# Scores of the first key block in two halves of 64 keys on four square tiles of TensorE

## The chip, the cores and the metric

The kernel runs on one core of one Trainium2 chip. The metric is the device time of one execution in microseconds. The kernel before was run three times: median 3692.19 us, from 3688.66 to 3693.34 us. A separate execution was profiled, and all views below are of that one.

## The reference, cut to what matters

The input is 32 sequences of 256 tokens with 256 channels. A conditioned state-space layer (projection, short convolution, a recurrence over the 256 tokens, gate, projection) is followed by two transformer layers of local attention and a gated feed-forward part. The change lies in the attention:

```python
        def local_attention(q, k, v):
            b, h, n, d = q.shape
            w = n // WINDOW
            ...
            sim = jnp.einsum('bhwid,bhwjd->bhwij', bq, bk)
            i = bt[:, :, None]
            j = btk[:, None, :]
            mask = (i < j) | (i > j + WINDOW) | (j == -1)
            sim = jnp.where(mask, -jnp.finfo(sim.dtype).max, sim)
            attn = jax.nn.softmax(sim, axis=-1)
            out = jnp.einsum('bhwij,bhwjd->bhwid', attn, bv)
```

There are 8 heads of 64 channels and WINDOW is 128, so the 256 tokens form two windows. A query `i` sees a key `j` only where `j <= i <= j + 128`. The first key block (keys 0 to 127) is therefore seen by queries of both windows, but its first half (keys 0 to 63) by queries 0 to 191 alone, and its second half (keys 64 to 127) by queries 64 to 255 alone. The second key block (keys 128 to 255) is seen by queries 128 to 255 alone.

## The kernel before, in words

The 32 sequences are handled in four groups of eight. For each group a scan runs over the 256 tokens (`group_scan`, line 376 on): every step is one VectorE operation `h` (L706), which needs a row block `xrep` that was fetched by a transfer on SP's queue (L675) and scaled by ScalarE (L696). Four steps are read out together by TensorE, each on its own tile of 32 columns (`y`, L718). The scan of a group runs beside the attention and feed-forward work of the group before it. The last group's attention and feed-forward have no scan beside them.

The order of the transformer work is written out by hand: `attend` and `feed` put the steps of each sequence into numbered stages (`stage(n, i, ...)`, eight stages per sequence), and a loop at the end of `program` plays the stages and advances the scan slot by slot between them. The build then arranges the instructions of each engine, so that an engine's queue is nearly, and not exactly, in this order. [...]

For each sequence the attention does this. `project` makes q, k and v of a window (L965). `turn` transposes q and k, so that in `qT` and `kT` the 64 channels of an even head lie in partitions 0 to 63 and those of the odd head beside it in partitions 64 to 127. `scores` takes a key block `kw`, a first head pair `i0` and a number `n` of head pairs; it makes keys-by-queries scores in two PSUM banks, one for the even heads (`r` = 0) and one for the odd (`r` = 1). The matmuls of `r` = 0 and `r` = 1 use the upper and lower 64 rows of the array, so they are two row tiles of 64 x 128. For the first key block it is called twice per sequence (stages 3 and 5), with two head pairs and 256 queries each; for the second once (stage 2), with four head pairs and 128 queries.

The mask comes in one of two ways. In the first three groups `self.apart` is false: a bf16 matmul of an identity with the mask (L1167) opens each bank with -32768 at every hidden place and 0 elsewhere, and the score matmuls (L1174) add to it. In the last group `self.apart` is true: the score matmuls write the bank themselves, and VectorE or GpSimd multiplies by a mask of ones and zeros after the exponential. In both ways ScalarE takes the exponential of the whole bank (L1183), 128 partitions by 512, into `pT`. `sums` (L1204, four column tiles of 32) and `values` (L1223, two column tiles of 64) then read `pT`.

A matmul on fp32 operands leaves two MATMUL records and two weight loads in the trace.

## Time and profile before

| What | Value |
|---|---|
| Median of three runs | 3692.19 us (3688.66 to 3693.34) |
| Span of the profiled execution | 3693.9 us |
| TensorE busy | 3580.5 us, 97%, 19804 matmul records |
| VectorE busy | 2714.2 us, 73% |
| ScalarE busy | 2163.0 us, 59% |
| GpSimd busy | 1812.1 us, 49% |
| Score matmuls of the first key block (L1174, 64x256) | 1024 records, 147.0 us busy, 406 ns mean |
| Score matmuls of the second key block (L1174, 64x128) | 1024 records, 74.4 us busy, 285 ns mean |
| Mask matmuls (L1167) | 288 records, 88.1 us busy, 383 ns mean |

The profiled execution's own time is its span, the time from the first to the last instruction; it is within 2 us of the median of the runs. Busy time counts moments in which an engine has at least one instruction in flight; TensorE overlaps its matmuls, and where two tiles of the array work together their records overlap too, so that a record's duration is longer than the time that it adds. The page divides the span into 40 slices of about 92 us and gives the busy share of each in tenths.

### The profile page before, as it was taken

What the parts mean: (1) busy time and instruction counts of PE and PEld (TensorE: products, weight loads), DVE (VectorE), ACT (ScalarE), POOL (GpSimd) and SP (SyncE); (2) the same over time, 40 slices, a digit from 0 to 9 for tenths busy, and PEclk for the clock granted to TensorE, in tenths of its full rate; (3) what the DMA queues carried; (4) which work ended last, traced back from release to release, by engine and by line L of the source; (5) the groups of instructions that cost most, each with busy time, mean ns of one, the idle gap of its engine ahead of it and who ended that gap; (6) DMA issues with size and microseconds to landing.
All of it is one profiled execution on the core that took longest, in us unless ns stands there. A gap on an engine that the chain in (4) does not pass through costs nothing.

```text
span 3693.9 us, 56916 instructions
## 1 busy us (share of the span) xinstructions
PE 3580.5 (97%) x19804; PEld 2234.3 (60%) x19804; DVE 2714.2 (73%) x5177; ACT 2163.0 (59%) x3689; POOL 1812.1 (49%) x1745
## 2 busy tenths in 40 slices
PE   7999989999999999999999999999999999999999
PEld 4444335666566566666666666666666666666666
DVE  5888889878787777877787778877777445455553
ACT  3666656666666666666666666666666444444442
POOL 4433366445455455545455556544554444444551
PEclk9999999999999999999999999999999999999999
DMA  7877655544454555444454555544453212011101
GB/s 196 209 201 206 185 164 148 134 110 135 124 139 119 140 141 145 131 112 124 119 138 124 135 145 138 134 111 130 111 134 114 59 35 59 12 30 39 30 27 36
DMA packets 469213, 435.80 MB, mean 118 GB/s; under 512 B 228835, under 2 KB 308532, under 8 KB 468788
## 3 DMA queue, kind: packets, MB, share of 16 engines
q1 hardware_dynamic: 384466, 420.05, 42.2%
q10 hardware_dynamic: 84450, 12.01, 2.1%
q8 instruction: 160, 2.62, 0.3%
q14 instruction: 137, 1.12, 0.1%
HBM read 383.70 MB, written 46.66 MB: 117 GB/s over the span
## 4 chain that ended last, share of the span: by engine, by line
PE 67%; DVE 15%; DMA 5%; POOL 5%; ACT 3%; issue 3%; SPq 0%; ACTq 0%; DVEq 0%; POOLq 0%
PE ps_qkv L965 13%; PE pa L1326 13%; PE po_f L1354 8%; DVE h L706 6%; PE y L718 5%; PE ps_wo L1015 4%; PE sc L1174 4%; DMA xrep<-xnd 4%; PE ov L1223 3%; PE ps_out L796 3%; PE ps_in L398 2%; PE tr_qk L1004 2%; DVE acc L488 2%; PE rs L1204 2%; ACT xrep L696 2%
## 5 line engine op out<-in xcount | busy, mean ns | idle before, releaser
L706 DVE CUSTOM_DVE_ANT_0 h<-h,xrep,lim 128x512 f32<-128x512 f32 x1024 | 947.3, 925 | 232.2 <-ACT xrep L696 197.5
L696 ACT ACTIVATE xrep<-xrep,beta 128x512 f32<-128x512 f32 x960 | 672.8, 719 | 336.1 <-DMA xrep<-xnd 239.0
L965 PE MATMUL ps_qkv<-qkv,res 128*128 128x512 f32 x1536 | 724.7, 607 | 19.2 <-DVE ag L1342 8.3
L1326 PE MATMUL pa<-hT,w 128*128 128x256 f32 (+1 forms) x3072 | 690.4, 387 | 1.6 <-ACT hT L1305 1.3
L1326 PEld LDWEIGHTS pa<-hT,w 128*128 128x128 f32 (+1 forms) x3072 | 493.8, 178 | 186.6 <-issue 77.8
L989 POOL TENSOR_TENSOR rot<-rot,swp 128x512 f32<-128x512 f32 x256 | 335.4, 1310 | 482.4 <-DVE swp L986 353.2
L965 PEld LDWEIGHTS ps_qkv<-qkv,res 128*128 128x128 f32 x1536 | 278.0, 191 | 328.9 <-issue 250.0
L997 POOL TENSOR_TENSOR rn<-ss,neg_half 128x8 f32<-128x8 f32 x256 | 459.2, 1794 | 15.6 <-DVE ss L995 5.4
L1354 PE MATMUL po_f<-ag,w 128*128 128x256 f32 (+1 forms) x1536 | 388.5, 394 | 11.5 <-DVE ag L1342 7.6
L1342 DVE SCALAR_TENSOR_TENSOR ag<-pa,b_sb,ag 128x256 f32<-128x256 f32 (+1 forms) x448 | 213.1, 476 | 234.4 <-ACT ag L1334 231.8
L718 PE MATMUL y<-h,ly 128*32 128x512 f32 x2048 | 357.1, 614 | 10.7 <-DVE h L706 7.9
L1279 POOL TENSOR_TENSOR rstd<-ve,neg_half 128x2 f32<-128x2 f32 x64 | 46.4, 724 | 614.8 <-DVE ve L1277 596.9
L1354 PEld LDWEIGHTS po_f<-ag,w 128*128 128x128 f32 (+1 forms) x1536 | 273.4, 189 | 119.5 <-issue 47.3
L998 POOL TENSOR_TENSOR rot<-rot,rn 128x512 f32<-128x512 f32 x256 | 291.0, 1137 | 20.1
L978 ACT ACTIVATE sq<-ps_qkv 128x512 f32<-128x512 f32 x256 | 151.9, 596 | 229.3 <-PE ps_qkv L965 181.0
L1334 ACT ACTIVATE ag<-pa,b_sb 128x256 f32<-128x256 f32 x320 | 150.4, 470 | 206.1 <-PE pa L1326 203.6
L488 DVE SCALAR_TENSOR_TENSOR acc<-xr,wc_sb,acc 128x256 f32<-128x256 f32 x384 | 192.7, 524 | 55.7 <-POOL acc L477 55.1
L1015 PE MATMUL ps_wo<-oT,wo 128*128 128x256 f32 x1024 | 231.7, 379 | 0.3 <-ACT ag L1334 0.2
L981 DVE TENSOR_TENSOR rot<-ps_qkv,rc_sb 128x512 f32<-128x512 f32 x256 | 174.8, 683 | 73.4 <-ACT sq L978 72.3
L1174 PE MATMUL sc<-qT,kT 64*128 64x128 f32 (+1 forms) x2048 | 221.3, 345 | 0.0
L1183 ACT ACTIVATE pT<-sc 128x512 f32<-128x512 f32 x384 | 208.6, 596 | 15.2 <-PE sc L1174 13.2
L1015 PEld LDWEIGHTS ps_wo<-oT,wo 128*128 128x128 f32 x1024 | 194.3, 190 | 28.2 <-ACT ag L1334 1.0
(153 smaller groups left out, 5493.7 us busy)
## 6 DMA issues: line engine op xcount, KB each, us to landing
xrep<-xnd SPq DMA_DIRECT2D x960, 256.0 KB
rb<-inv SPq DMA_DIRECT2D x128, 256.0 KB
xnd<-xn SPq DMA_DIRECT2D x64, 256.0 KB
qkv<-in_wqkv_dram SPq DMA_DIRECT2D x24, 512.0 KB
ahead<-xs_a SPq DMA_DIRECT2D x48, 256.0 KB
xp<-ahead SPq DMA_DIRECT2D x48, 256.0 KB
xd<-xnd SPq DMA_DIRECT2D x192, 64.0 KB
w<-in_w_dram SPq DMA_DIRECT2D x80, 128.0 KB
```

What stands on the lines that cost most here:

```text
L488: nc.vector.scalar_tensor_tensor(acc, xr[:, :, k : k + CH], wc_sb[:, ch, k : k + 1], acc, ALU.mult, ALU.add,)
L696: scaled = nc.scalar.activation(bx, ck[c].pop(("bx", t), bx), AF.Copy, scale=ck[c]["beta"][:, t : t + 1])
L706: nc.vector._custom_dve(TENSOR_ADD_SAT, out=h_new, in0=state["h"], in1=bx, s0=ck[c]["lim"][:, 0, t : t + 1], s1=ck[c]["lim"][:, 1, t : t + 1],
L718: nc.tensor.matmul(ck[c]["y", hb][32 * q : 32 * q + 32, :], ly[hb % 2][:, 32 * t : 32 * t + 32], ck[c].pop(("h", hb * TB + t)), start=(i = ...
L965: nc.tensor.matmul(ps, res[b][:, k, t0 : t0 + W], wt["qkv", a][:, k], start=(k == 0), stop=(k == KM - 1),)
L989: nc.gpsimd.tensor_add(rot, rot, swp)
L997: nc.gpsimd.tensor_tensor(rn, ss, neg_half, ALU.pow)
L998: nc.gpsimd.tensor_mul(rot, rot, bc(rn, 2, DH))
L1015: nc.tensor.matmul(po[:, d], wt["wo", 0][:, c, d * P : (d + 1) * P], oT[:, c, :], start=(c == 0), stop=(c == NC_ - 1),)
L1174: nc.tensor.matmul(banks[r][:, i, :], kT[rows, i0 + i, kw * W : (kw + 1) * W], qT[rows, i0 + i, kw * W :], start=self.apart, stop=self.apa ...
L1326: nc.tensor.matmul(pg if x else pa, wt["w1", m][:, k, x], self.h[:, k], start=(k == 0), stop=(k == KM - 1),)
L1354: nc.tensor.matmul(self.po[:, d], wt["w2", 0][r0 : r0 + n, m, d * P : (d + 1) * P], self.ag[m][r0 : r0 + n], start=(m == 0), stop=(m == le ...
```

## The change

In `scores`, for the first key block and where the mask was added by TensorE, each matmul of 128 keys by 256 queries is replaced by two matmuls. The first takes keys 0 to 63 with queries 0 to 191 and writes partitions 0 to 63 of the bank; the second takes keys 64 to 127 with queries 64 to 255 and writes partitions 64 to 127. Together with the two row halves (even and odd heads) this addresses the array as four tiles of 64 x 64. The places that no matmul adds to any more (keys 0 to 63 with queries 192 to 255, and keys 64 to 127 with queries 0 to 63) are hidden ones, and keep the mask value that the mask matmul wrote. The second key block and the last group run as before. In the changed file the score matmul stands in line 1181, and later lines are seven further down.

```diff
+                halved = kw == 0 and not self.apart
+                nm = 2 if halved else 1
+                mk = W // nm
                 for i in range(n):
                     for r in range(2):
                         rows = slice(r * DH, (r + 1) * DH)
-                        nc.tensor.matmul(
-                            banks[r][:, i, :],
-                            kT[rows, i0 + i, kw * W : (kw + 1) * W],
-                            qT[rows, i0 + i, kw * W :],
-                            start=self.apart,
-                            stop=self.apart or i == n - 1,
-                        )
+                        for m in range(nm):
+
+                            k0 = m * mk
+                            q0, q1 = (k0, k0 + W + mk) if halved else (0, nq)
+                            nc.tensor.matmul(
+                                banks[r][k0 : k0 + mk, i, q0:q1],
+                                kT[rows, i0 + i, kw * W + k0 : kw * W + k0 + mk],
+                                qT[rows, i0 + i, kw * W + q0 : kw * W + q1],
+                                start=self.apart,
+                                stop=self.apart or i == n - 1,
+                            )
                 for r in range(2):
```

## The prediction

> **What bounds the kernel now.** I read the page first: the busy shares, the chain of waits, the slices.

> ```profile
> span 3693.9 us, 56916 instructions
> PE 3580.5 (97%) x19804; PEld 2234.3 (60%) x19804; DVE 2714.2 (73%) x5177; ACT 2163.0 (59%) x3689; POOL 1812.1 (49%) x1745
> ...
> PE   7999989999999999999999999999999999999999
> PEclk9999999999999999999999999999999999999999
> ...
> PE 67%; DVE 15%; DMA 5%; POOL 5%; ACT 3%; issue 3%; SPq 0%; ACTq 0%; DVEq 0%; POOLq 0%
> ```

> TensorE is busy almost throughout and holds 67% of the chain; no other engine passes 73%. A busy TensorE includes modelled ends, so I checked the part that the change touches with the view of busy time by stretches. The first score block of 256 queries starts at 535 us, and the groups with an added mask end by 2995 us:

> ```profile
> 532.00:1500.00 968.00, 935.64 (x5373) 0.99 0.50 132
> 1500.00:2995.00 1495.00, 1481.88 (x8582) 1.00 0.45 120
> ```

> TensorE idles 32.4 of 968 us in the first stretch (3.3%) and 13.1 of 1495 us in the second (0.9%). Its longest named waits there are for VectorE, 8.3 us at most in sum for one pair. So TensorE sets the pace, tightly in the second stretch, less so in the first.

> Next the groups of the view by form, and one block in the timeline, cut into stretches of 0.2 us so that records in flight together are listed apart (start us, length us, engine, line, form, count):

> ```profile
> L1174 PE MATMUL sc<-qT,kT 64*128 64x256 f32 x1024 | 147.0, 406 | 0.0
> ...
> 1508.18 0.49 PE L1174 MATMUL sc<-qT,kT 64*128 64x256 f32 x2
> 1508.50 0.81 PE L1174 MATMUL sc<-qT,kT 64*128 64x256 f32 x6
> 1508.93 0.38 PE L1174 MATMUL sc<-qT,kT 64*128 64x256 f32 x2
> 1509.24 0.64 PE L718 MATMUL y<-h,ly 128*32 128x512 f32 x4
> 1509.69 0.61 PE L718 MATMUL y<-h,ly 128*32 128x512 f32 x4
> 1510.24 0.48 PE L1326 MATMUL pa<-hT,w 128*128 128x256 f32 x1
> ...
> 1518.87 1.51 PE L1204 MATMUL rs<-pT,head_cols 128*32 128x256 f32 x32
> 1520.31 3.17 PE L1223 MATMUL ov<-pT,v_sb 128*64 128x256 f32 x32
> ```

> Each fp32 matmul leaves two records[...] (8 for the four score matmuls of a block, 2048 for the 1024 read-outs `y`, one a scan step). The block of four matmuls costs 1508.18 to 1509.24 = 1.06 us from its first record to the next work; the single records show that all 96 blocks of the masked groups have a median of 1064 ns. Two records, one per row tile, start 6 ns apart and run together. The read-out `y` shows the same for four column tiles: eight 512-column records in 1.00 us, where one after another they would take 8 x 0.427 = 3.4 us. There is no idle time before the group: operands are there.

> [...]

> **A formula for a block.** Within `sc`, single records show the second pair 320 ns after the first, further pairs 215 ns apart, and the next work 306 ns after the last record. So a pass of 256 columns takes 213 ns, the first weight load (128 columns) adds 107, a change of mode adds 93. For four 32-column tiles of 512 the second group comes 453 ns after the first: 427 + 27. For the two 64-column tiles of `ov` it comes 266 later: 213 + 53. The exposed load follows the columns of one tile, and tiles load side by side. Check on `rs`: 27 + 4 x 216 + 4 x 109 + 20 stagger + 94 = 1441 ns, and the timeline has 1518.87 to 1520.31 = 1.44 us.

> **The change, part by part.**

> *Removed and added on TensorE.* 96 blocks (3 groups x 2 layers x 8 sequences x 2) lose four matmuls 64x256 and gain eight 64x192 on four tiles: 768 more records and as many weight loads. A pass of 192 columns lies between 109 (128) and 216 (256): 162 ns. A new block, if the four tiles run together: 53 (first load, 64 columns) + 4 groups x 162 + 20 (stagger) + 94 (mode) = 815 ns. Gain 1064 - 815 = 249 ns a block, 23.9 us in all. Issue is no bound on this: `rs` issues four 128-column matmuls with their loads per 109 ns, here there are 162 ns for four. The bounds of the untried: best, also the 53 and the stagger hide, 740 ns, gain 31 us; worst, the two column halves of a row tile run in turn, 8 x 163 + 53 + 94 = 1451 ns, loss 387 ns a block, 37 us. I take 815, since both kinds of packing are seen and share one array.

> *Mask and exp.* The mask matmul (L1167) still opens the whole bank, so a corner no longer added to keeps -32768, exp of which is 0. Mode changes stay: before, the block already stood between a full-array mask matmul and other full- or column-tile work. Exp (L1183) reads the same 128x512 bank, 0.25 us earlier; it is of no use to it, as it waited only 17.6 us for scores in the whole span. No wait is added: both built programs have 3021 matmuls that wait. Not touched: the first 532 us and the last group (32 blocks after 2995 us).

> *Order.* Elsewhere the built programs stand in nearly the same order. On TensorE six instructions move; they cut `y` runs (306 runs after, 303 before). A run cut off costs its own two passes, 2 x 427 + 27 + 94 = 975 ns[...]: 3 x 1.0 to 1.2 = about 3 us. On VectorE some 119 of 5180 instructions stand elsewhere, by a few places, on ScalarE 42, GpSimd 57, on SP's queue 44, nearly all transfers of scan rows `xrep`. They are issued in the same number; I cost this at nothing, covered by TensorE's backlog, and give it 3 us either way.

> *What of it reaches the end.* A saving passes until TensorE meets a wait that doesn't move with it. In 1500 to 2995 us, 59 blocks, idle 0.9%: I take 90%: 59 x 0.249 x 0.9 = 13.2 us. In 532 to 1500 us, 37 blocks, idle 3.3%: VectorE's scan chain (waits `h` <- `xrep` <- transfer) paces some of it; I take 65%: 37 x 0.249 x 0.65 = 6.0 us. Sum 19.2, less 2.5 for order: 16.7 us. From the profiled span 3693.9 this gives 3677.2. The three runs have a median of 3692.2, 1.7 below the profiled execution, so 3675.5; I say 3675.

> **Rivals.**

> *The gain is swallowed.* VectorE (some 400 of 500 us busy between 1000 and 2500) or the scan rows' transfers become the pace; TensorE's idle grows by most of 23.9 us. For it: the chain of waits between 1490 and 1533 us runs through VectorE, GpSimd, a transfer and ScalarE without TensorE. Against: in that stretch TensorE itself had hardly a gap. A third of the gain, 8 us less 3 for order: about 3687.

> *The column halves run in turn.* In each row tile, the second half waits for the first. Place: the new block at each of 96 sites. Price 387 ns each, 3692 + 37 = 3729. It decides from a block of 1064 + 77 = 1141 ns up (7.4 us over 96), that is a group of four in 243 ns instead of 162. For it: no trace shows a row and a column split at once. Against: `y` streams four different operands from all 128 partitions into four tiles at full pace, more than this needs.

> *The order loses more than I count.* Shifted scan transfers or a later VectorE step open waits of some 15 to 20 us more than counted: 3692 to 3697, no change.

> **How the numbers follow.** Main case 0.70, around 3675, own range 3665 to 3684. Swallowed 0.14 (3684 to 3691). In turn 0.09 (3729). Order 0.07. 0.2% is 7.4 us, about what a measurement of this kernel can tell from no change: 3685 and 3700 are the bounds. Faster: 0.70 and nearly half of the swallowed, 0.76. Same: the rest of it and most of the order case, 0.13. Slower: 0.11. The range 3664 to 3690 leaves out the case in turn, some of the order case, and a full pass-through with all loads hidden (3692 - 31 = 3661).

> **What would show it.** Right: 20572 matmul records; a group of form 64*64, 64x192, x1536; four of its records starting within some 25 ns, groups 162 ns apart, a block in about 0.82 us; the gain lying between 532 and 2995 us, the time from there to the end unchanged near 699 us; TensorE idle in 532 to 2995 us up from 45.5 to about 50 us. Wrong: blocks near 1.45 us (in turn), or blocks of 0.82 us with idle up by 15 us or more (swallowed).

## The result, and the profile after

The changed kernel takes 3676.17 us in the median of five runs (3672.99 to 3681.02); the kernel before took 3691.43 us in five runs (3688.66 to 3693.34). The ratio is 0.9959, with a 95% interval of 0.9948 to 0.9970: 15 us faster. The profiled execution of the changed kernel spans 3679.2 us, and is the slowest of its five runs.

The page after, the parts that answer to those shown of before (span; busy times; slices of TensorE and its clock; the chain):

```profile
span 3679.2 us, 58433 instructions
PE 3560.8 (97%) x20572; PEld 2218.3 (60%) x20572; DVE 2708.4 (74%) x5177; ACT 2161.1 (59%) x3689; POOL 1819.4 (49%) x1745
...
PE   7999989999999999999999999999999999999999
PEclk8999999999999999999999999999999999999999
...
PE 66%; DVE 16%; DMA 5%; POOL 5%; ACT 4%; issue 3%; SPq 0%; ACTq 0%; DVEq 0%; POOLq 0%
```

TensorE's busy time fell by 19.7 us, the busy time of VectorE, ScalarE and GpSimd moved by less than 8, and the chain shifted by one point from TensorE to VectorE and ScalarE. TensorE, busy for 97% of the span and with 66% of the chain, is still the engine that sets the pace.

The new matmuls in the view by form, and one block in the timeline, cut into short stretches so that records in flight together are listed apart (start us, length us, engine, line, form, count):

```profile
L1181 PE MATMUL sc<-qT,kT 64*64 64x192 f32 x1536 | 85.9, 339 | 0.0
...
1501.56 0.39 PE L1181 MATMUL sc<-qT,kT 64*64 64x192 f32 x4
1501.78 0.67 PE L1181 MATMUL sc<-qT,kT 64*64 64x192 f32 x12
1502.10 0.34 PE L1181 MATMUL sc<-qT,kT 64*64 64x192 f32 x4
1502.37 0.64 PE L718 MATMUL y<-h,ly 128*32 128x512 f32 x4
```

Four records start together at 1501.56, on the four tiles; the last four start at 1502.10, and the next work at 1502.37, 0.81 us after the block began. Over the 96 blocks the single records give a median of 811 ns, where it was 1064. From first record to next work the 96 blocks took 105.6 us in the trace before and 80.4 us in this one: TensorE got 25 us back in these places, and the span fell by 14.7.

**Where the rest went.** TensorE's queue holds the same matmuls in nearly the same order in both kernels, so the start of each can be set against its start before. How far ahead the changed kernel is, at the same score matmul:

| Time in the kernel before, us | 533 | 669 | 1276 | 1500 | 1997 | 2975 | end |
|---|---|---|---|---|---|---|---|
| Ahead by, us | 1.0 | -2.9 | 5.1 | 6.8 | 8.5 | 14.2 | 14.7 |

Each block gains 0.25 us. Between 533 and 669 us nearly 4 us are lost all the same, and from 1276 us on, where 68 blocks give back 17.2 us, only 9.6 arrive. The last 699 us are the same in both (TensorE busy 691.4 us after, 691.1 before).

The early loss is one stall, at 622 us (timeline after, TensorE; in brackets the idle time before it and what ended it):

```profile
622.03 1.92 PE L718 MATMUL y<-h,ly 128*32 128x512 f32 x2 [4.31 <-DVE h L706]
```

A read-out of the scan waits 4.31 us for the scan step that it reads. In the kernel before no read-out waits longer than 0.5 us between 600 and 640 us. This read-out is one of the few TensorE instructions that the build moved: it was cut off from its run and put behind the mask matmuls. The place of the read-out isn't what costs, though: it stands later in TensorE's queue than before, and still waits. The step that it reads was moved too, on VectorE. Before, then after (VectorE; `rot` belongs to the rotation of q and k):

```profile
614.57 0.80 DVE L706 CUSTOM_DVE_ANT_0 h<-h,xrep,lim 128x512 f32<-128x512 f32 x1
615.29 0.68 DVE L981 TENSOR_TENSOR rot<-ps_qkv,rc_sb 128x512 f32<-128x512 f32 x1
```

```profile
616.20 0.69 DVE L981 TENSOR_TENSOR rot<-ps_qkv,rc_sb 128x512 f32<-128x512 f32 x1 [0.84 <-ACT sq L978]
...
619.23 0.69 DVE L981 TENSOR_TENSOR rot<-ps_qkv,rc_sb 128x512 f32<-128x512 f32 x1 [1.09 <-ACT sq L978]
...
621.17 0.81 DVE L706 CUSTOM_DVE_ANT_0 h<-h,xrep,lim 128x512 f32<-128x512 f32 x1
```

Before, the step `h` runs ahead of the rotations; after, it stands behind two of them in VectorE's queue, which themselves wait for ScalarE, and it ends at 621.98 us. Behind the stall TensorE is also slow for a while: the next block takes 1.48 us (623.88 to 625.36) in place of 0.81, and the mean granted clock from 532 to 680 us is 0.94, where it was 0.98.

The steady loss shows in the waits of TensorE between 1276 and 2985 us (who waited for whom: us in total, times, longest). Before, then after:

```profile
PE ps_qkv L965 <- DVE ag L1342: 8.3, 12, 1.2
PE sc L1167 <- DVE ag L1342: 4.7, 7, 0.9
PE ps_qkv L965 <- DVE rinv L1212: 1.9, 3, 0.9
```

```profile
PE ps_qkv L965 <- DVE ag L1349: 8.0, 11, 0.9
PE sc L1167 <- DVE ag L1349: 6.7, 8, 1.0
PE ps_qkv L965 <- DVE rinv L1219: 3.1, 6, 0.9
```

These are waits for a PSUM bank: the kernel passes TensorE's results through eight PSUM tiles in turn (`ps_w`, `bufs=8`), and in the program a mask matmul or a projection into a tile depends on VectorE's reading of the tile's last contents (`ag`, `rinv`). One of them in the timeline after (VectorE and TensorE):

```profile
2019.81 0.47 DVE L488 SCALAR_TENSOR_TENSOR acc<-xr,wc_sb,acc 128x256 f32<-128x256 f32 x1
2019.83 0.38 PE L1167 MATMUL sc<-mask_t,ident_b 128*128 128x512 bf16 x1
...
2020.39 0.42 DVE L471 TENSOR_TENSOR xr<-xp,cond_sb 128x256 f32<-128x256 f32 x1
2020.73 0.48 DVE L1349 SCALAR_TENSOR_TENSOR ag<-pa,b_sb,ag 128x256 f32<-128x256 f32 x1
...
2021.26 0.38 PE L1167 MATMUL sc<-mask_t,ident_b 128*128 128x512 bf16 x1 [1.05 <-DVE ag L1349]
```

The second mask matmul of the block stands 1.05 us and starts at 2021.26, when `ag` has emptied its bank (2020.73 + 0.48 = 2021.21), and `ag` stands in VectorE's queue behind the convolution of the scan's next chunk. At the same place before, TensorE came later and waited 0.6 us. TensorE's waits in this stretch grew by 4 us in all; starts that slip by 0.1 to 0.3 us inside the modelled end of the previous matmul, mostly at the second half of `values`, account for most of the other 3 to 4. That TensorE waits longer because it arrives earlier is one reading of this. It doesn't fit every wait: see the waits of `two` and `wide` below.

### The profile page after: what moved, and what is told of

It reads as the page before. It is cut to its first block, busy times and chain, and to the rows that moved or that the text cites. A ratio compares the mean times of both kernels' runs of the same rounds, so it can differ in the third digit from the quotient of the medians.

```text
span 3679.2 us, 58433 instructions
## 1 busy us (share of the span) xinstructions
PE 3560.8 (97%) x20572; PEld 2218.3 (60%) x20572; DVE 2708.4 (74%) x5177; ACT 2161.1 (59%) x3689; POOL 1819.4 (49%) x1745
## 2 busy tenths in 40 slices
PE   7999989999999999999999999999999999999999
## 4 chain that ended last, share of the span: by engine, by line
PE 66%; DVE 16%; DMA 5%; POOL 5%; ACT 4%; issue 3%; SPq 0%; ACTq 0%; DVEq 0%; POOLq 0%
PE ps_qkv L965 14%; PE pa L1333 13%; PE po_f L1361 7%; DVE h L706 6%; PE y L718 5%; PE ps_wo L1015 4%; DMA xrep<-xnd 4%; PE sc L1181 4%; PE ov L1230 4%; PE ps_out L796 3%; PE ps_in L398 2%; PE tr_qk L1004 2%; DVE acc L488 2%; PE rs L1211 2%; ACT xrep L696 2%
## 5 line engine op out<-in xcount | busy, mean ns | idle before, releaser
L696 ACT ACTIVATE xrep<-xrep,beta 128x512 f32<-128x512 f32 x960 | 673.4, 719 | 342.3 <-DMA xrep<-xnd 245.5
L718 PE MATMUL y<-h,ly 128*32 128x512 f32 x2048 | 358.1, 611 | 14.6 <-DVE h L706 13.0
L1015 PE MATMUL ps_wo<-oT,wo 128*128 128x256 f32 x1024 | 231.7, 379 | 0.5 <-ACT ag L1341 0.5
L1015 PEld LDWEIGHTS ps_wo<-oT,wo 128*128 128x128 f32 x1024 | 194.3, 190 | 28.4 <-ACT ag L1341 1.2
L1181 PE MATMUL sc<-qT,kT 64*64 64x192 f32 (+2 forms) x2816 | 196.6, 325 | 0.0
```

The lines of the kernel that those rows point to most:

```text
L696: scaled = nc.scalar.activation(bx, ck[c].pop(("bx", t), bx), AF.Copy, scale=ck[c]["beta"][:, t : t + 1])
L718: nc.tensor.matmul(ck[c]["y", hb][32 * q : 32 * q + 32, :], ly[hb % 2][:, 32 * t : 32 * t + 32], ck[c].pop(("h", hb * TB + t)), start=(i = ...
L1015: nc.tensor.matmul(po[:, d], wt["wo", 0][:, c, d * P : (d + 1) * P], oT[:, c, :], start=(c == 0), stop=(c == NC_ - 1),)
L1181: nc.tensor.matmul(banks[r][k0 : k0 + mk, i, q0:q1], kT[rows, i0 + i, kw * W + k0 : kw * W + k0 + mk], qT[rows, i0 + i, kw * W + q0 : kw * ...
```

## The experiments

Ratios are to the kernel before, run on the same chip between the runs, with 95% intervals.

| Run | What it is | Median us | Ratio | Block, ns |
|---|---|---|---|---|
| the change | halves on four tiles | 3676.2 | 0.9959 (0.9948 to 0.9970) | 811 |
| late | halves from the fourth sequence on | 3674.2 | 0.9952 (0.9939 to 0.9966) | 811 |
| two | fewer queries only (leaves out scores that are needed) | 3674.8 | 0.9950 (0.9936 to 0.9964) | 851 |
| wide | four tiles only | 3694.7 | 1.0006 (0.9998 to 1.0014) | 1024 |
| quarters | eight tiles, 160 queries | 3667.9 | 0.9935 (0.9921 to 0.9948) | 704 |
| relief_before | kernel before, less work on VectorE (leaves out one convolution tap and the reciprocal) | 3682.7 | 0.9976 (0.9968 to 0.9983) | 1064 |
| relief_after | the change, the same left out | 3660.7 | 0.9911 (0.9897 to 0.9925) | 811 |
| turns | the change, tile by tile | 3691.5 | 0.9997 (0.9987 to 1.0007) | 831 |
| before_turns | kernel before, in that order | 3725.9 | 1.0080 (1.0066 to 1.0094) | 1071 |
| before_turns_fix | the same, ScalarE's queue put in order | 3664.8 | 0.9921 (0.9907 to 0.9934) | 1071 |
| turns_fix | turns, the same | 3653.8 | 0.9897 (0.9882 to 0.9913) | 831 |
| tail | quarters, halves in the last group too | 3654.7 | 0.9897 (0.9884 to 0.9910) | 704 and 811 |
| tail_fix | tail, ScalarE's queue put in order | 3632.7 | 0.9839 (0.9825 to 0.9852) | 704 and 811 |

### What shortens a block: fewer columns or more tiles

```diff
 two:
-                nm = 2 if halved else 1
+                nm = 1
-                            q0, q1 = (k0, k0 + W + mk) if halved else (0, nq)
+                            q0, q1 = 0, nq - 64 if halved else nq
 wide:
-                            q0, q1 = (k0, k0 + W + mk) if halved else (0, nq)
+                            q0, q1 = 0, nq
 quarters:
-                nm = 2 if halved else 1
+                nm = 4 if halved else 1
```

> Only the queries are cut: 128 keys with queries 0 to 191 on the two row tiles of before (the scores of keys 64 to 127 with queries 192 to 255 are left out and stay at the mask's 0). Theory (the gain comes from 192 columns in place of 256, the four tiles are only what makes this possible): a block in 107 + 4 x 162 + 7 + 94 = 856 ns, TensorE saves 20 us, about 3679 us. Rival (the gain comes from the number of tiles at work): a block stays near 1064 ns and the time near 3691 us.

> Only the tiles are split: 64 keys with all 256 queries on four square tiles. Theory: a block in 53 + 4 x 216 + 20 + 94 = 1031 ns, 33 ns less than before, TensorE saves 3 us, 3689 to 3691 us. Rival (four tiles at work gain by themselves): a block near 811 ns and the time near 3676 us.

> The split is taken further: four quarters of 32 keys with 160 queries each, on eight tiles of 64 x 32. Theory: a pass of 160 columns takes 135 ns, a block 27 + 4 x 135 + 47 stagger + 94 = 708 ns, 103 ns less than in halves, TensorE saves 10 us more, of which some 60% pass: about 3670 us. Rival (the rate of issue bounds it, as four records and their loads take 109 ns in the row sums): groups of eight every 218 ns, a block in 27 + 4 x 218 + 47 + 94 = 1040 ns, time near 3690 us.

The forms of the new matmuls in `two`, `wide` and `quarters`, one line from each view by form:

```profile
L1181 PE MATMUL sc<-qT,kT 64*128 64x192 f32 x768 | 90.4, 355 | 0.0
```

```profile
L1181 PE MATMUL sc<-qT,kT 64*64 64x256 f32 x1536 | 106.5, 393 | 0.0
```

```profile
L1181 PE MATMUL sc<-qT,kT 64*32 64x160 f32 x3072 | 75.4, 306 | 0.0
```

The blocks came out at 851, 1024 and 704 ns, where the formula of the prediction gave 856, 1031 and 708. So the gain of a block is that of the columns: cutting the queries alone, without more tiles, gives 213 of the 253 ns; the four tiles alone give 40, which in the formula is the shorter first weight load (54) less the longer stagger (13). The tiles are there so that no score that is needed is left out, as some are in `two`. The eight tiles of `quarters` ran together as well: the eight records of a group start 7 ns apart, and the groups follow at 136 ns. The rival for `quarters`, groups every 218 ns by a bound on issue, is out.

In the whole time the three don't follow their blocks so neatly. From 1276 us on, by the start times in one profiled execution each, `two` keeps 12.7 us of 68 x 0.213 = 14.5, `quarters` 18.5 of 24.5, the change 9.6 of 17.2, and `wide` loses 1.6 where it should gain 2.7. Their queues differ from that of the changed kernel, by some 40 to 100 instructions on VectorE and by up to some 20 on ScalarE. This was the first sign that the order there is worth several microseconds. The mask matmul's wait for `ag` between 1276 and 2960 us says the same: it is 4.7 us before and 6.7 in the changed kernel, but 4.4 in `two`, which gains nearly as much in each block, and 6.2 in `wide`, which gains next to nothing. So this wait doesn't follow the gain; the order on VectorE is a rival cause for this part of the loss, and no run here holds it fixed.

### The moved instructions

```diff
-                halved = kw == 0 and not self.apart
+                halved = kw == 0 and not self.apart and self.n >= 3
```

(`self.n` is the number of the sequence.)

> The halves are used from the fourth sequence on (90 blocks instead of 96); TensorE's queue then stands exactly as before, apart from the score matmuls. Theory (the six moved TensorE instructions, a read-out put ahead of others, cost some 4 us between 532 and 680 us): no stall of several us near 618 us, start of the eighth sequence about 2 us ahead of before where the changed kernel is 3 us behind, and 3672 to 3674 us in all. Rival (that loss is chance[...]): the six blocks less cost 1.5 us, 3677 to 3678 us.

The stall is not there: between 600 and 640 us the longest wait of a read-out is 0.5 us, and from 533 to 669 us `late` gains 0.3 us against the kernel before where the change loses 3.9. The same stall, 2.7 to 4.5 us, stands at 617 to 622 us in `two`, `wide`, `quarters`, `turns` and `tail`, which have the read-out moved too. In these five too the scan step runs behind both rotations. So the traces show that the loss goes with the move of the step and of its read-out; `late` undoes both at once. The medians of 3674.2 and 3676.2 us have intervals that overlap, so in the whole time it isn't resolved. The start of the eighth sequence was no good test: `late` was already 4.2 us behind at 533 us, ahead of its first score block. Where nothing was changed, executions of these kernels lie from 4.2 us behind to 6.0 us ahead at that point, so one trace alone is good for no less than some 5 us up to there.

### Who takes the steady loss

```diff
-                for k in range(1, TAPS):
+                for k in range(1, TAPS - 1):
                     nc.vector.scalar_tensor_tensor(
...
-                nc.vector.reciprocal(rinv, rs)
+                nc.vector.tensor_copy(rinv, rs)
```

> The kernel before with less work on VectorE: the last of three convolution taps is left out and the reciprocal of the softmax sums is a plain copy, so the values differ; some 150 us of VectorE's 2714 fall away. It is the base for the run after it: below the kernel before by what its waits for VectorE cost, 3660 to 3685 us. By itself it tells nothing between the theories.

> The changed kernel with the same work left out. Theory (in the steady stretch the gain is lost where TensorE, now earlier, waits for a PSUM bank that VectorE gives back late, since VectorE's queue is nearly full there): against the base the difference grows from 15 us to 20 to 24 us, and from 1276 to 2975 us before most of 64 x 0.253 = 16 us passes instead of 9. Rival (the loss has nothing to do with VectorE): the difference stays near 15 us, and 9 of 16 pass.

The pair differs by 3682.7 - 3660.7 = 22.0 us, and from 1276 us on the two traces draw apart by 17.3 us, all that 68 blocks give. The waits of TensorE in that stretch of `relief_after`:

```profile
PE ps_qkv L965 <- DVE ag L1349: 7.1, 10, 0.9
PE ps_wo L1015 <- ACT ag L1341: 2.7, 5, 1.2
PE ps_qkv L965 <- ACT oT L1237: 1.8, 5, 0.7
PE ps_qkv L965 <- DVE swp L986: 1.0, 1, 1.0
```

No mask matmul (L1167) waits any more, and no projection for `rinv`, in either of the two. In this pair the whole gain arrives; in the changed kernel 44% of it is lost in this stretch, while `two` loses 12% and `quarters` 24%. The pair doesn't say how much of that is VectorE's load: leaving work out also made the build arrange the queues anew. Against the kernel before, some 400 instructions on VectorE, 70 on ScalarE and 50 matmuls stand elsewhere in `relief_before`. Note that the relief itself brought the kernel before only 10 us for some 150 us of VectorE's work: VectorE isn't the pace, it is late at some hand-overs.

### The order of the matmuls in a block

```diff
-                for i in range(n):
-                    for r in range(2):
+                order = [(i, r, m) for i in range(n) for r in range(2) for m in range(nm)]
+                if halved:
+                    order.sort(key=lambda x: x[1:])
+                for i, r, m in order:
```

> The changed kernel with the score matmuls of a block in another order: both head pairs of one tile, then the next tile. Theory (tiles run together only while the queue brings different tiles in a row): a tile's four passes come one after another and little runs together, a block of up to 53 + 16 x 162 + 94 = 2.7 us, which would add up to 180 us; with half of it together, some 70 us. Rival (TensorE takes a free tile's matmul from further back): a block stays at 811 ns and the time near 3676 us.

The block is 831 ns: the rival was right on this. Four passes (a pass here is one of the two records that a matmul leaves) still start together, 13 ns apart, though the fourth tile's first pass stands twelve passes further back in the queue. By these times (16 passes of 162 ns one after another would take 2.6 us) work for a free tile was taken from there. But the time is 3691.5 us, and of 22 us nothing arrives. TensorE's queue is that of the changed kernel apart from the order within these blocks. Its waits between 1276 and 2960 us:

```profile
PE ps_qkv L965 <- DVE ag L1352: 11.5, 12, 1.6
PE tr_qk L1004 <- DVE ag L1352: 11.2, 12, 1.2
PE sc L1167 <- DVE ag L1352: 6.3, 7, 1.0
```

The second line is new. I took it first for an effect of VectorE's order, since in the built program 30 of 448 products `ag` stand on the other side of a scan step, and tested whether it needs the four tiles at all:

```diff
 before_turns, against turns:
-                nm = 2 if halved else 1
+                nm = 1
-                            q0, q1 = (k0, k0 + W + mk) if halved else (0, nq)
+                            q0, q1 = 0, nq
```

> The kernel before, its score matmuls of 128 keys by 256 queries unsplit, in the order of the run turns (both head pairs of the even heads, then of the odd). TensorE's queue is otherwise as before; on VectorE 32 of the 448 feed-forward products stand on the other side of a scan step, as in turns. Theory (in turns the place of those products behind a scan step, which waits for its row, cost the whole gain): TensorE waits for `ag` at the transposes L1004 for 10 to 14 us between 1276 and 2985 us, and the time is 3702 to 3708 us. Rival (the loss in turns has to do with the four tiles): no such waits, blocks 10 to 30 ns longer, 3692 to 3695 us.

It needs no tiles: 3725.9 us, 30 us slower than the kernel before with blocks 7 ns longer, twice what I expected. The transposes wait 10.7 us for `ag`, as foretold, and the projections a further 21.7 us for `rinv`. The place of `ag` doesn't explain that, so I looked at what `ag` itself waits for. At one of these transposes in `turns` (timeline: ScalarE, VectorE, TensorE):

```profile
2038.22 0.72 ACT L696 ACTIVATE xrep<-xrep,beta 128x512 f32<-128x512 f32 x1 [2.40 <-DMA xrep<-xnd]
2038.85 0.56 ACT L1009 COPY qT<-tr_qk 128x512 f32<-128x512 f32 x1
2039.32 0.58 ACT L1009 COPY kT<-tr_qk 128x512 f32<-128x512 f32 x1
...
2040.42 0.47 ACT L1344 ACTIVATE ag<-pa,b_sb 128x256 f32<-128x256 f32 x1
2040.56 0.81 DVE L706 CUSTOM_DVE_ANT_0 h<-h,xrep,lim 128x512 f32<-128x512 f32 x1 [4.55 <-ACT xrep L696]
...
2041.28 0.48 DVE L1352 SCALAR_TENSOR_TENSOR ag<-pa,b_sb,ag 128x256 f32<-128x256 f32 x1
...
2041.91 0.63 PE L1004 MATMUL tr_qk<-ident,rot 128*128 128x128 f32 x4 [1.13 <-DVE ag L1352]
```

and at the same place in the changed kernel:

```profile
2034.65 0.56 ACT L1009 COPY qT<-tr_qk 128x512 f32<-128x512 f32 x1
2035.12 0.59 ACT L1009 COPY kT<-tr_qk 128x512 f32<-128x512 f32 x1
2035.59 0.73 ACT L696 ACTIVATE xrep<-xrep,beta 128x512 f32<-128x512 f32 x1
2037.16 0.72 ACT L696 ACTIVATE xrep<-xrep,beta 128x512 f32<-128x512 f32 x1 [0.84 <-DMA xrep<-xnd]
2037.79 0.46 ACT L1341 ACTIVATE ag<-pa,b_sb 128x256 f32<-128x256 f32 x1
```

In `turns` ScalarE's queue has the scaling of a scan row ahead of the copies of q and k. The row's transfer isn't there, ScalarE stands for 2.40 us, and the copies, which free two banks, and the Gelu `ag`, on which VectorE's `ag` waits, stand behind it. In the changed kernel the copies come first. VectorE's order has a smaller part in it: `ag` could have started when ScalarE's Gelu ended at 2040.89, and started at 2041.28, behind the scan step. In the built programs 30 of the 256 copies stand behind one row more than in the kernel before in `turns`, 28 in `before_turns`, and 2 in the changed kernel. So I held the rows back: in the next edit each scaling of a row depends on the last copy that the kernel's text puts ahead of it (an edge for the build, which then can't put the row first).

```diff
 turn():
-            nc.scalar.copy(dst, tr)
+            last_copy[0] = nc.scalar.copy(dst, tr)
 scale_row():
                     tc.keep_in_program_order(scaled)
+                    if last_copy[0] is not None:
+                        tc.add_manual_dep(
+                            scaled.ins, last_copy[0].ins.name,
+                            mybir.DependencyInfo(
+                                mybir.DependencyClass.NoSync, mybir.DependencyReason.DATA
+                            ),
+                            reason="behind the copies",
+                        )
```

> As before_turns, but on ScalarE every scaling of a scan row (L696) stays behind the copies of q and k that the kernel's text puts ahead of it; in before_turns 28 of the 256 copies stand behind one row scaling more than in the kernel before, here none does, and 157 stand further ahead. TensorE's queue is otherwise the same. Theory (before_turns lost 30 us since ScalarE, waiting for a row's transfer, held back the copies that free TensorE's banks): 3680 to 3700 us, and the waits of the transposes L1004 for `ag` gone. Rival (another of the moved instructions is the cause, on VectorE): 3715 us or more.

> As turns, with the same rule on ScalarE. Theory: the gain of the shorter blocks arrives, 3660 to 3680 us. Rival: it stays near 3691 us.

3725.9 became 3664.8 us, and 3691.5 became 3653.8: both below the changed kernel. ScalarE's waits for a row's transfer between 1276 and 2960 us were 87.8 us before and 95.5 us in the changed kernel; in `before_turns`:

```profile
ACT xrep L696 <- DMA xrep<-xnd: 142.4, 42, 5.8
```

In `before_turns_fix` no such wait is left among the waits of that stretch, and TensorE's are these three:

```profile
PE sc L1177 <- DVE ag L1362: 4.8, 7, 1.3
PE ov L1243 <- DVE ag L1362: 0.7, 2, 0.4
PE ps_wo L1025 <- ACT ag L1354: 0.2, 1, 0.2
```

So holding the rows back on ScalarE is enough to undo what `before_turns` lost, and the timelines show how a row ahead of the copies does harm. That ScalarE's order alone is the cause isn't shown. The edge names ScalarE only, but the build followed it on VectorE: by the traces some 160 instructions stand elsewhere there, and in the built programs 16 of the 448 products `ag` stand behind one scan step more than in the kernel before in `before_turns`, and none in `before_turns_fix`. The edge also does more than undo the loss: 157 copies now stand ahead of rows that they stood behind in the kernel before, and the kernel gains 28 us with blocks of the old size. What the edge doesn't restore is the passing of the gain. Between `before_turns_fix` and `turns_fix` lie 11.0 us, and their blocks differ by 96 x 0.240 = 23 us, so half is lost here too. The wait of the mask matmul for `ag` grows from 4.8 to 6.8 us; where the rest of this loss lies isn't shown.

### A faster version

```diff
 tail, against the change:
-                halved = kw == 0 and not self.apart
-                nm = 2 if halved else 1
+                halved = kw == 0
+                nm = (2 if self.apart else 4) if halved else 1
...
-                    nc.scalar.activation(p, banks[r], AF.Exp)
+                    if self.apart and halved:
+                        for m in range(nm):
+                            k0, q0 = m * mk, m * mk
+                            s = slice(k0, k0 + mk), slice(None), slice(q0, q0 + W + mk)
+                            nc.scalar.activation(p[s], banks[r][s], AF.Exp)
+                    else:
+                        nc.scalar.activation(p, banks[r], AF.Exp)
...
+                    if kw == 0:
+                        nc.vector.memset(p[0:DH, :, S - DH :], 0.0)
+                        nc.vector.memset(p[DH:P, :, 0:DH], 0.0)
```

> Quarters in the masked groups, and halves on four tiles also in the last group: there the exponential is taken in two pieces of 64 partitions by 2 x 192, and VectorE clears the two corners of each bank before the mask is multiplied. Theory (after 2980 us TensorE alone sets the pace, so everything passes): 32 blocks x 253 ns = 8 us below the quarters, about 3660 us. Rival (the longer exponentials and the clearing delay the products behind them, and the sums wait): the last 699 us stay or grow, 3668 us or more.

> As tail, with the same rule on ScalarE. Theory (rows scaled later cost nothing while TensorE sets the pace, and copies out of the way help): 3645 to 3655 us. Rival (later rows delay the scan, and VectorE with it): 3660 us or more.

`tail` takes 3654.7 us. Its profiled execution gains 0.5 us with every sequence of the last group, 8.1 us from 3016 us to the end: there everything passes, and the longer exponentials (two of 485 ns where one took 597, in the trace of `tail_fix`) cost nothing that shows. With the same edge on ScalarE, `tail_fix` takes 3632.7 us (3626.8 to 3635.4), 1.6% below the kernel before and the fastest of all that ran.

## Why the prediction was right, and where it was wrong

The time was forecast at 3675 us and is 3676.2.

**The block.** 815 ns was worked out, 811 measured, and the single records fit the four terms (weight load 53, passes of 162, stagger 20, mode change 94): 213 ns from the first group to the second and 162 between the later ones, so 51 for the load; 20 within a group; 253 from the last record to the next work, so 91 for the change of mode. The trace before shows that last term at other lines too: a record of 128x256 is followed 216 ns later by one of the same tile form (L1326 to L1015, 62 places), and 309 ns later by one of another (L1326 to L1204, 62 places). Records, form and count are as listed: 20572, 64*64, x1536. The rival "in turn" is out.

**The order.** About three microseconds were reckoned for the moved read-outs, and 2.5 entered the sum; of the 1.0 to 1.2 us for each, 975 ns come from records and the rest was my estimate. The traces show one stall of 4.3 us and 3.9 us lost up to 669 us. The size was about right, by luck, and the mechanism wrong: I priced the extra passes of a read-out cut off from its run, and what cost was a wait for a scan step that the build had put behind the rotations on VectorE. That is a reordering on VectorE, which I had put at nothing.

**What reaches the end.** This step failed, and its two errors canceled out; that the sum came within 2 us is luck. I took 90% for 1500 to 2995 us since TensorE was idle there for 0.9% of the time, and 65% for the looser stretch ahead of it. By the start times, the second stretch passed 7.9 of 59 x 0.253 = 14.9 us, 53%. The first gained 5.8 us net; without the early stall, from 669 to 1500 us, it gained 9.7 us, more than its 31 blocks give (7.8). So the tight stretch lost and the loose one did not. The waits were in the rows I read and put aside: a queue with little idle time can still be one whose banks come back just in time. With VectorE relieved, and the queues in another order, the whole gain arrives in the same stretch; how much of the loss is TensorE's arriving earlier and how much the new order on VectorE stays open. The rival "the gain is swallowed" comes nearest, with about half its size. Its mechanism as written doesn't hold: VectorE did not become the pace, and TensorE's idle time didn't grow by most of 23.9 us.

**Idle time.** It was to rise from 45.5 to about 50 us; it is 30.2 + 17.4 = 47.6 us (968 - 937.8 and 1480 - 1462.65 in the view by stretches). It fits, and tells little: it rose by 4.3 us in the second stretch and fell by 2.2 in the first, and slips inside modelled ends don't count as idle.

**What I hid at no cost.** The reordering on the other engines was costed at nothing with 3 us either way. In the change itself it already cost the 3.9 us above, and perhaps part of the later loss. And `before_turns` shows what it can do: with TensorE's work the same, 28 copies behind one row more on ScalarE and some 95 instructions in other places on VectorE went with a loss of 30 us. A range of 3 us for it had no ground in the profile; it was luck that the build left the copies on ScalarE nearly alone here.

## What to carry to other kernels

Here the cut of moving columns paid by the columns on a TensorE that was 97% busy (213 of the 253 ns of a block), and the blocks could be priced to within 1% from records of other packings in the same trace (815, 856, 1031 and 708 ns against 811, 851, 1024 and 704). How much of it arrives depended here on the hand-overs: before taking a share of the gain, look at who gives back the bank that the next matmul waits for, and what stands ahead of that instruction in its queue. After any edit under a scheduler compare the built order on all engines, and look first for an instruction that waits for a transfer and now stands ahead of one that frees a buffer.
